# One group-norm chain for all four channel blocks in the last element of a two-layer attention kernel

## The chip, the cores and the metric

The kernel runs on one core of a Trainium2 chip. The metric is the device time of one execution in microseconds (us), as the median of three runs. Beside these runs there is one profiled execution with a trace; its span is the time from its first to its last recorded instruction.

The core's engines each have a queue of their own and work in its order: TensorE (PE, with its weight loads shown apart as PEld), VectorE (DVE), ScalarE (ACT), GpSimd (POOL) and SyncE (SP), which here only issues DMAs.

## The reference, cut to what matters

The input is eight images ("elements") of 512 channels and 32 x 32 = 1024 positions, in float32. Two attention layers follow each other; every element is computed by itself.

```python
# layer 0
hn  = group_norm(x, gn1_scale, gn1_bias)          # 32 groups of 16 channels
qkv = w_qkv @ hn + b_qkv                          # 8 heads of 64 channels
a   = softmax(q^T k / 8) applied to v, per head
out = w_proj @ a + b_proj
x   = x + group_norm(out, gn2_scale, gn2_bias)    # the second group norm
# layer 1: one head of 512 channels, with rows of weights normed and q, k, v divided by their rms
x   = (x + w_out @ attention(x)) / sqrt(2)
```

A group norm takes mean and variance over the 16 channels of a group and all positions, and then scales and shifts each channel. The change concerns the group norm of `out` and the sum with `x` at the end of layer 0.

## The kernel before

**Tiling.** The 512 channels are four blocks of 128 partitions (`CI` = 4); block j of a tile is `t[:, j, :]`, 128 x 1024. The positions fall into two halves of 512 (`th`), the width of one matmul. A float32 matmul shows as two records in the trace.

**Order of the work.** The order is written out by hand. Every engine is wrapped in `InOrder` (line 26), which pins each engine's instructions to the program's order, so all of them carry line 34 in the profile and are told apart by the names of their tiles. The loop over elements runs layer 0's heads in 32 steps, then the end of layer 0, then layer 1. In all elements but the last, the end of layer 0 is `finish_layer0` (line 691), which has matmuls of the next element to put between its steps. The last element has no next one, and ends layer 0 in another way.

**The last element's end of layer 0.** Its output projection is taken in shares. `project_out_half` (line 508) has already written the shares of blocks 0 and 1 of `a`, with the bias, into `o`, while the heads still ran. `OutBegun` (line 517) then starts the sums of block 2 of `a` for three of the four output blocks, in three PSUM tiles `pp` (all that the pool `ps_s`, line 101, has). After the last heads' values, `finish_last` (line 528) adds the rest: `project_out(j, th, pm)` gives PE the last share of output block j, and DVE adds the PSUM tile to `o`. Output block 3 was not begun; it takes both shares at once, and its PSUM tile is that of block 0, free when block 0 has been added to `o`.

**The second group norm, before.** In `finish_last` it is one chain for each block of channels, with one column each. `norm(j)` takes the statistics (two `bn_stats`, one `bn_aggr`, tiles `st` and `mv`). `GroupNorm.mean_steps` (line 261) lets PE average over the groups with a matmul against `gavg` (PSUM tile `pm`), and DVE does four small steps (`mean`, `d` three times). `GroupNorm.coeff_steps` (line 276) averages again on PE (`pv`); DVE adds the epsilon (`ve`), finds the reciprocal root by a start value and three rounds of four steps (`rsqrt_steps`, line 191), and ends with `a` and `c`. Then ACT applies `a` and `c` to block j of `o`, and DVE adds the block to `x`. The chains are interleaved with the projections: in round j, the first half of block j's projection comes first in the code, then the coefficients and the activation of block j-2, then the second half, the add of block j-2 to `x`, the add of block j to `o`, the means of block j-1, and the statistics of block j. The last two blocks' remains follow behind the loop, with the fetch of `gram` between them.

**What comes behind it.** `fetch("gram", b)` issues on SP the load of layer 1's first weights into the buffer that the projection's weights held (`places`, line 209: both have the tag `p`), so it waits for the last projection. `fetch("value", b)` (line 1092) comes next on SP. `Layer1.project` (line 750) starts with the products `py` of `gram` and `x`, block by block: output block cj takes blocks 0 to cj of `x`, 20 matmuls in all. DVE takes sums and differences of `x` (`RightSide.sums`, line 584) and multiplies `py` by `x` into `xy`, from which the rms comes. The products `p_u`, `p_v`, `p_e` and `po` follow.

Of the kernel before, what the change touches and what calls it, by code (L numbers as in the profile page):

```python
# [8 lines left out]
F32 = mybir.dt.float32  # L9
I32 = mybir.dt.int32  # L10
AF = mybir.ActivationFunctionType
ALU = mybir.AluOpType
AX = mybir.AxisListType
P = 128
# [4 lines left out]
G1S, G1B, BQ, BK, BV, BP, G2S, G2B, GQKV, GOUT, NCOLS = 0, 4, 8, 12, 16, 20, 24, 28, 32, 44, 48  # L19
# [33 lines left out]
def attention_blocks_kernel(  # L53
# [29 lines left out]
    CI, NT, HN = C // P, N // P, N // 2  # L83
# [15 lines left out]
    small = ctx.enter_context(tc.tile_pool(name="small", bufs=3))  # L99
# [4 lines left out]
    PE, VE, AC, PO, SY = (InOrder(tc, e) for e in (nc.tensor, nc.vector, nc.scalar, nc.gpsimd, nc.sync))  # L104

    def big(name, lead=CI):

        return slots.take([P, lead, CI * N // lead], name)

    def wide(name):  # L110
        return ps_s.tile([P, 2, HN], F32, tag="sc", name=name)
# [4 lines left out]
    def matmuls(pm, terms):  # L116

        for k, (lhsT, rhs) in enumerate(terms):
            PE.matmul(pm, lhsT, rhs, start=(k == 0), stop=(k == len(terms) - 1))
            if k % 2:  # L120
                yield

    def run(pieces):
        for _ in pieces:
            pass
# [105 lines left out]
    def fetch(name, b):  # L231
        SY.dma_start(out=place(name, b), in_=far[name])
# [16 lines left out]
    def gn_stats(st, src, k):  # L249
        VE.bn_stats(st[:, k, :], src[:, k * HN : (k + 1) * HN])  # L250
# [253 lines left out]
    def out_terms(a, j, th, cis):  # L504
        hs = slice(th * HN, (th + 1) * HN)
        return [(near["proj"][:, ci, j * P : (j + 1) * P], a[:, ci, hs]) for ci in cis]
# [21 lines left out]
    def finish_last(b, h, xt, o, begun):  # L528

        def project_out(j, th, pm):
            terms = out_terms(h.a, j, th, range(CI // 2, CI))
            if j in begun.pm:
                PE.matmul(pm[:, th, :], *terms[1], start=False, stop=True)
            else:
                run(matmuls(pm[:, th, :], terms))

        norms = {}

        def norm(j):
            st = small.tile([P, 2, 6], F32, tag="gn_st2", name=f"st2_{b}_{j}")
            mv = small.tile([P, 1, 2], F32, tag="gn_mv2", name=f"mv2_{b}_{j}")
            for k in range(2):
                gn_stats(st, o[:, j, :], k)
            VE.bn_aggr(mv[:, 0, :], st)
            norms[j] = GroupNorm(mv, 1, G2S + j, G2B + j, f"2_{b}_{j}")

        def apply(j):
            a, c = norms[j].coeffs()  # L550
            AC.activation(o[:, j, :], o[:, j, :], AF.Identity, bias=c, scale=a)

        def add(j):
            VE.tensor_add(xt[:, j, :], xt[:, j, :], o[:, j, :])

        for j in range(CI):
            pm = begun.pm[j] if j in begun.pm else wide(f"pp_{b}_{j}")
            project_out(j, 0, pm)
            if j > 1:
                apply(j - 2)  # L560
            project_out(j, 1, pm)
            if j > 1:
                add(j - 2)
            VE.tensor_add(o[:, j, :], o[:, j, :], pm.rearrange("p a f -> p (a f)"))
            if j:
                norms[j - 1].means()
            norm(j)
        apply(CI - 2)
        fetch("gram", b)
        add(CI - 2)  # L570
        norms[CI - 1].means()
        apply(CI - 1)
        add(CI - 1)
        slots.give(f"a_{b}")
        slots.give(f"o_{b}")

# [444 lines left out]
    for b in range(B):  # L1021
        hn, more = heads.hn, b + 1 < B
        todo = iter(())
        for i in range(STEPS):
            j, r = divmod(i, NB)
# [17 lines left out]
            if more:  # L1043
# [9 lines left out]
                k = i - 3 * CI - 2  # L1053
# [9 lines left out]
            if i == STEPS - NB + 1:  # L1063
                xt = big(f"x_{b}")
# [23 lines left out]
        if more:  # L1088
            finish_layer0(b, heads, rhs, xt, v0)
        else:  # L1090
            finish_last(b, heads, xt, o_last, begun)
# [59 lines left out]
```

## Time and profile before

| what | value |
|---|---|
| median of three runs | 3327.03 us (3325.53, 3327.03, 3331.03) |
| the profiled execution | 3326.53 us |
| its span | 3324.7 us |
| mean clock granted to PE in it | 0.997 |
| end of layer 0 of the last element, from the first add of `pp` to `o` until `py` starts | 3113.92 to 3144.45 us of the span |
| first products of layer 1 (`py`) | 3144.45, for 19.36 us |

The page gives busy times of the engines and groups of instructions. The answers from the trace give single instructions: start in the span, duration, engine, line, operation, output and inputs by name with their sizes, how often, and in brackets how long the engine was idle before and what ended that. An operation shown with 128x1 works on one column, with 128x4 on four.

### The profile page before, as it was taken

Reading aid. Unit: us, or ns where it says so; the run is one execution under the profiler, and the core shown is the slowest. Engines: PE = TensorE matmul, PEld = TensorE weight load, DVE = VectorE, ACT = ScalarE, POOL = GpSimd, SP = SyncE. Lnnn points to the kernel's source line nnn. Section 1 sums busy time; section 2 is a strip of 40 time slices with the busy share of each in tenths; the row PEclk is TensorE's granted clock in tenths of the full one; section 3 lists DMA queues with packets and bytes.
Section 4 is the critical chain, followed back from the end, with each engine's and each line's share of the span. In section 5 each row is a group of like instructions: output and inputs, shape, how many; then the busy total and the mean of one; then the engine's idle time right before and its main releaser. Section 6 shows DMA issues by size and latency. Waiting matters only on the chain.

```text
span 3324.7 us, 35644 instructions
## 1 busy us (share of the span) xinstructions
PE 3270.4 (98%) x13189; PEld 1608.1 (48%) x13189; DVE 2127.5 (64%) x2893; ACT 1069.8 (32%) x1811; POOL 981.4 (30%) x855
## 2 busy tenths in 40 slices
PE   7999999999999999999999999999999999999799
PEld 3544544445444454444544445444544445444354
DVE  4596646965479554885449754596646965478653
ACT  2353123521245212451215412254123531245210
POOL 0253123521245112450224503254123521234111
PEclk9999999999999999999999999999999999999899
DMA  5586205751068410782118811387204752067400
GB/s 187 160 212 189 76 13 155 195 176 67 7 185 209 147 45 26 204 224 95 45 50 217 236 47 44 88 216 199 76 13 142 200 166 93 5 159 203 151 7 25
DMA packets 182659, 411.86 MB, mean 124 GB/s; under 512 B 27444, under 2 KB 27480, under 8 KB 176344
## 3 DMA queue, kind: packets, MB, share of 16 engines
q1 hardware_dynamic: 182368, 409.58, 43.3%
q8 instruction: 105, 1.72, 0.2%
q14 instruction: 66, 0.54, 0.0%
q10 hardware_dynamic: 120, 0.02, 0.0%
HBM read 113.53 MB, written 27.56 MB: 42 GB/s over the span
## 4 chain that ended last, share of the span: by engine, by line
PE 86%; DVE 6%; DMA 5%; SPq 2%; issue 1%; ACT 0%; DVEq 0%; POOL 0%; POOLq 0%; ACTq 0%
PE po L34 24%; PE pqk L34 11%; PE s L34 11%; PE pv L34 7%; PE p_e_T L34 7%; PE p_e_B L34 5%; DMA pT<-pb 5%; PE py L34 4%; PE p_u_T L34 3%; PE p_o_T L34 3%; PE p_v_T L34 2%; PE p_u_B L34 2%; DVE pb L34 2%; PE p_o_B L34 2%; PE p_v_B L34 2%; SPq L34 2%
## 5 line engine op out<-in xcount | busy, mean ns | idle before, releaser
L34 ACT ACTIVATE p<-s,nm 128x1024 f32<-128x1024 f32 x512 | 565.5, 1109 | 861.3 <-DVE nm L34 825.7
L34 POOL TENSOR_SCALAR p<-p,tt 128x1024 f32<-128x1024 f32 x512 | 565.9, 1118 | 927.3 <-DVE tt L34 923.9
L34 DVE TENSOR_REDUCE nm<-s 128x1 f32<-128x1024 f32 x512 | 602.6, 1219 | 176.3 <-PE s L34 175.1
L34 DVE STREAM_TRANSPOSE pb<-p 128x2048 f32<-128x2048 f32 x256 | 589.6, 2303 | 23.2 <-POOL p L34 18.7
L34 PE MATMUL s<-qk 64*128 64x512 f32 x2048 | 508.1, 602 | 0.0
L34 PE MATMUL po<-pT,v 128*64 128x256 f32 x4096 | 470.3, 382 | 4.1 <-DMA pT<-pb 2.6
L34 PE MATMUL pqk<-hn,qk 64*128 64x512 f32 (+1 forms) x2016 | 473.9, 591 | 0.0
L34 PE MATMUL po<-e,v 128*128 128x512 f32 x1024 | 450.9, 595 | 0.0
L34 PEld LDWEIGHTS po<-pT,v 128*64 128x64 f32 x4096 | 286.7, 137 | 216.4 <-ACT v L34 71.3
L34 PEld LDWEIGHTS pqk<-hn,qk 64*128 64x128 f32 (+1 forms) x2016 | 201.8, 187 | 252.1 <-issue 239.7
L34 PEld LDWEIGHTS po<-e,v 128*128 128x128 f32 x1024 | 192.2, 190 | 252.7 <-issue 245.5
L34 POOL TENSOR_TENSOR u<-u,xy 128x512 f32<-128x512 f32 x64 | 78.9, 1270 | 781.3 <-DMA xy<-far_rinv 781.3
L34 PEld LDWEIGHTS s<-qk 64*128 64x128 f32 x2048 | 193.3, 186 | 238.6 <-issue 235.1
L34 PE MATMUL pv<-v,hn 128*128 128x512 f32 x512 | 230.7, 602 | 1.4 <-ACT v L34 1.4
L34 DVE TENSOR_TENSOR e<-e,p_e_T 128x512 f32<-128x512 f32 x160 | 107.1, 686 | 145.0 <-PE p_e_T L34 142.8
L34 POOL TENSOR_TENSOR qk<-qk,v 128x512 f32<-128x512 f32 x124 | 158.3, 1277 | 83.9 <-ACT v L34 83.9
L34 ACT ACTIVATE e<-e,shift,rinv 128x512 f32<-128x512 f32 x128 | 100.9, 811 | 247.7 <-DVE e L34 247.7
L34 POOL TENSOR_TENSOR esum<-esum,e 128x512 f32<-128x512 f32 x96 | 121.5, 1267 | 163.9 <-ACT e L34 161.4
L34 PEld LDWEIGHTS pv<-v,hn 128*128 128x128 f32 x512 | 95.3, 191 | 117.8 <-issue 116.0
L34 PE MATMUL p_e_T<-s,t 128*128 128x512 f32 x320 | 147.8, 592 | 0.0
L34 DVE TENSOR_TENSOR v<-po,esum 128x512 f32<-128x512 f32 x56 | 38.7, 691 | 160.0 <-PE po L34 159.8
L34 PE MATMUL py<-x,gram 128*128 128x512 f32 x320 | 140.7, 599 | 0.0
(184 smaller groups left out, 3077.8 us busy)
## 6 DMA issues: line engine op xcount, KB each, us to landing
pT<-pb SPq DMA_DIRECT2D x1024, 256.0 KB, 4.6
hn<-in_x_dram SPq DMA_DIRECT2D x32, 512.0 KB, 5.5
x<-in_x_dram SPq DMA_DIRECT2D x32, 512.0 KB, 5.8
out_dram<-x SPq DMA_DIRECT2D x32, 512.0 KB, 4.0
score<-far_score SPq DMA_DIRECT2D x8, 1792.0 KB, 7.5
value<-far_value SPq DMA_DIRECT2D x8, 1792.0 KB, 7.1
qk<-far_qk SPq DMA_DIRECT2D x7, 2048.0 KB, 8.1
proj<-far_proj SPq DMA_DIRECT2D x7, 1792.0 KB, 8.4
```

Source lines behind the costliest of these rows:

```text
L34: return lambda *args, **kw: self._pin(call(*args, **kw))
```

## The change

The four chains become one. In the loop over j, PE gets both halves of block j's projection one after the other, DVE adds the PSUM tile to `o` and takes the statistics of block j, into the columns of one `st` and one `mv` tile. Behind the loop come the fetch of `gram`, then one `GroupNorm` with four columns (one `pm`, one `pv`, each small DVE step once, 128 x 4), and last, for each block, the activation on ACT and the add to `x` on DVE. What is computed stays the same.

```diff
-        norms = {}
-
-        def norm(j):
-            st = small.tile([P, 2, 6], F32, tag="gn_st2", name=f"st2_{b}_{j}")
-            mv = small.tile([P, 1, 2], F32, tag="gn_mv2", name=f"mv2_{b}_{j}")
-            for k in range(2):
-                gn_stats(st, o[:, j, :], k)
-            VE.bn_aggr(mv[:, 0, :], st)
-            norms[j] = GroupNorm(mv, 1, G2S + j, G2B + j, f"2_{b}_{j}")
-
-        def apply(j):
-            a, c = norms[j].coeffs()
-            AC.activation(o[:, j, :], o[:, j, :], AF.Identity, bias=c, scale=a)
-
-        def add(j):
-            VE.tensor_add(xt[:, j, :], xt[:, j, :], o[:, j, :])
-
+        st = small.tile([P, CI, 2, 6], F32, tag="gn_st2", name=f"st2_{b}")
+        mv = small.tile([P, CI, 2], F32, tag="gn_mv2", name=f"mv2_{b}")
         for j in range(CI):
             pm = begun.pm[j] if j in begun.pm else wide(f"pp_{b}_{j}")
-            project_out(j, 0, pm)
-            if j > 1:
-                apply(j - 2)
-            project_out(j, 1, pm)
-            if j > 1:
-                add(j - 2)
+            for th in range(2):
+                project_out(j, th, pm)
             VE.tensor_add(o[:, j, :], o[:, j, :], pm.rearrange("p a f -> p (a f)"))
-            if j:
-                norms[j - 1].means()
-            norm(j)
-        apply(CI - 2)
+            for k in range(2):
+                gn_stats(st[:, j], o[:, j, :], k)
+            VE.bn_aggr(mv[:, j, :], st[:, j])
         fetch("gram", b)
-        add(CI - 2)
-        norms[CI - 1].means()
-        apply(CI - 1)
-        add(CI - 1)
+        norm = GroupNorm(mv, CI, G2S, G2B, f"2_{b}")
+        norm.means()
+        a, c = norm.coeffs()
+        for j in range(CI):
+            AC.activation(o[:, j, :], o[:, j, :], AF.Identity, bias=c[:, j : j + 1], scale=a[:, j : j + 1])
+            VE.tensor_add(xt[:, j, :], xt[:, j, :], o[:, j, :])
         slots.give(f"a_{b}")
         slots.give(f"o_{b}")
```

## The prediction

> **What bounds the kernel now.** I read the page first. Its busy line says that PE sets the time: it works in 98% of the span. So a stretch in which PE waits is worth its full length, as far as nothing later takes it back.
>
> ```profile
> PE 3270.4 (98%) x13189; PEld 1608.1 (48%) x13189; DVE 2127.5 (64%) x2893; ACT 1069.8 (32%) x1811; POOL 981.4 (30%) x855
> ```
>
> The change lies in the end of element 7 (the last one), so I then asked for busy time by stage around it. Columns: the stretch, its length, busy time and instructions of PE, PEld, DVE, ACT and POOL, the clock granted to PE, the DMA share and GB/s.
>
> ```profile
> 3112.00:3123.00 11.00, 8.44 (x22) 3.27 (x22) 8.30 (x29) 0.47 (x1) 0.00 (x0) 1.00 0.04 13
> 3123.00:3144.00 21.00, 5.44 (x12) 3.13 (x12) 15.48 (x57) 3.72 (x3) 0.00 (x0) 0.62 0.35 137
> 3144.00:3164.00 20.00, 20.00 (x43) 9.11 (x44) 14.81 (x32) 1.24 (x1) 0.00 (x0) 0.89 0.00 0
> ```
>
> From 3123 to 3144 us PE is busy for 5.44 of 21 us, and part of that is at half clock. DVE is busy for 15.48. This is one of the few places where PE does not set the pace. The timeline there (start, duration, engine, operation, idle time before and what ended it) tells why; I cut it to what the sums use:
>
> ```profile
> 3113.92 1.22 DVE L34 TENSOR_TENSOR o<-o,pp 128x1024 f32<-128x1024 f32 x1 [12.72 <-PE pp L34]
> 3115.17 1.29 DVE L34 BATCH_NORM_STATS2 st<-o 128x6 f32<-128x512 f32 x2
> 3116.49 0.21 DVE L34 BATCH_NORM_AGGREGATE mv<-st 128x2 f32<-128x12 f32 x1
> 3116.62 1.17 DVE L34 TENSOR_TENSOR o<-o,pp 128x1024 f32<-128x1024 f32 x1
> 3116.85 0.35 PE L34 MATMUL pm<-mv,gavg 128*128 128x1 f32 x2 [1.25 <-DVE mv L34]
> ...
> 3143.21 0.15 DVE L34 COPY mean<-pm 128x1 f32<-128x1 f32 x1
> ...
> 3144.00 0.58 PE L34 MATMUL pv<-d,gavg 128*128 128x1 f32 x2 [5.76 <-DVE d L34]
> ...
> 3144.45 19.36 PE L34 MATMUL py<-x,gram 128*128 128x512 f32 x40
> 3144.62 0.16 DVE L34 TENSOR_SCALAR ve<-pv 128x1 f32<-128x1 f32 x1 [0.68 <-PE pv L34]
> ...
> 3147.96 1.24 ACT L34 ACTIVATE o<-o,c,a 128x1024 f32<-128x1024 f32 x1 [5.92 <-DVE c L34]
> 3149.23 1.22 DVE L34 TENSOR_TENSOR x<-x,o 128x1024 f32<-128x1024 f32 x1 [1.37 <-ACT o L34]
> ```
>
> DVE's one queue holds four such chains one after the other. The tiny matmuls pm and pv of each stand in PE's queue ahead of what follows, so PE waits for DVE's queue. PE reaches py, the first product of the next layer, only behind the last pv at 3144.00. By then blocks 0 to 2 of x are ready; py runs through although block 3 of x is added only at 3149.23. So what sets the end is: DVE's chains, pv of block 3, py, and PE from there on. The chain of waits agrees: it goes through DVE and ACT from 3113.92 to 3143.79, then through pv, py, p_u and on along PE.
>
> **What the Trainium skill says.** "VectorE: DVE Perf Modes", section "The TRN2 errata — SBUF-src ops pay a fixed extra latency per instruction", says that a short operation costs a fixed time per instruction, whatever its width. The trace agrees: the small steps take 0.16 us with 1 column and 0.16 with 4. "TensorE: Matmul & The Clock Gate", Part 1, says that the clock is halved after an idle window of about 3.4 us and full again after about as much work. The trace agrees: behind a 5.76 us gap, py's first weight loads start 0.85 us apart, and 0.43 apart from 3148.63 on.
>
> **The change part by part.**
>
> *Removed.* Three of four chains. Each has 4 DVE steps before pv (mean, d three times) and 17 behind it (ve, one start value, 12 steps of refinement, 3 for a and c): 21 instructions every 0.193 us, 4.05 us; three are 12.2 us of DVE. Also three of four DVE waits for ACT between c and the add of x (1.31, 1.31, 1.37, 1.37 us; together 5.4), some 4 us. On PE, six of eight tiny matmuls go; what matters is that none stands between the projections.
>
> *The new path, clock by clock, from the same first instruction.*
> 1. PE: the projections' 20 records follow at 0.43 us. The first 8 end at 3115.6 as before; 12 more end at 3120.8. Block 3 needs the PSUM buffer that the add of block 0 frees at 3115.14, earlier than its turn at 3117.3: no wait.
> 2. DVE: add, two statistics and the aggregate of one block take 3116.62 - 3113.92 = 2.70 us. Block 3's aggregate starts at 3113.92 + 3 x 2.70 + 2.57 = 3124.59 and ends at 3124.80. The adds of blocks 2 and 3 fall at 3119.3 and 3122.0, later than their matmuls (3117.3 and 3120.8), so DVE never waits for PE here.
> 3. pm 0.15 us later as in block 0: 3124.95. I take the half-clock 0.62 us from pv to ve (3144.00 to 3144.62) for it: PE has been idle for 4.1 us. The copy of mean starts at 3125.57.
> 4. From that copy to pv: 3144.00 - 3143.21 = 0.79; pv at 3126.36, ve at 3126.98.
> 5. ve to ACT with one column: 3147.96 - 3144.62 = 3.34. Element 6 has the same chain with four columns:
>
> ```profile
> 2747.87 0.17 DVE L34 TENSOR_SCALAR a<-ve 128x4 int32<-128x4 int32 x1
> ...
> 2751.05 4.64 ACT L34 ACTIVATE o<-o,c,a 128x1024 f32<-128x1024 f32 x4 [2.48 <-DVE c L34]
> 2752.32 4.63 DVE L34 TENSOR_TENSOR x<-x,o 128x1024 f32<-128x1024 f32 x4 [1.31 <-ACT o L34]
> ```
>
> There it is 3.18 us from the start value to ACT, and 0.20 before it: 3.38. ACT starts at 3130.36.
> 6. The add of x block 0 comes 1.27 later, at 3131.63, and ends at 3132.85. PE starts py at about 3132.95 (0.1 for the hand-over is my allowance; aggregate to pm shows 0.15, d to pv 0.05).
>
> py starts 3144.45 - 3132.95 = 11.5 us earlier. Blocks 1 to 3 of x follow every 1.14 us (4.63 for four), the last ready at 3136.2. py's four records on block 0 alone last 4 x 0.85 = 3.4 us, to 3136.35: the later adds hide there. Without that cover py would wait up to 3.4 us.
>
> *The clock.* In the kernel before, pv opens PE's work at 3144.00 and full clock comes some 4.4 us later. In the new one py itself opens it, so about 0.45 us more of py is at half clock: 0.2 us lost. Gain left: **11.3 us**.
>
> *DVE beside py.* It must finish xy and the sums of each block. In element 6, where the adds also come in a bunch beside py, it waits for py before the products of blocks 1, 2 and 3 (0.51, 0.86 and 2.58 us). DVE is not the limit.
>
> *Moved DMAs.* SP's queue holds gram (1 MB) and then value (1.8 MB):
>
> ```profile
> 3131.54 0.33 SPq L34 DMA_DIRECT2D gram<-far_gram  x1
> 3131.97 0.38 SPq L34 DMA_DIRECT2D value<-far_value  x1
> ```
>
> gram takes the buffer of the projection weights and can start when their last matmul is done: 3131.5 before, about 3120.8 now, 10.7 us earlier. In the kernel before the DMA engines are quiet from 3140.0 on, so both transfers need at most 8.5 us: 3129.3 now, 3.6 us ahead of py. If gram alone came late, each microsecond past 3132.9 would be one. value is needed by p_v (3189.04 before); it moves 10.7 us and its user 11.3, with 49 us of slack. No issue passes another on SP.
>
> *Behind py* every step is the same as before and starts from py: p_u, the square sums, the two small transfers of 1/rms, value and weight products. PE carries all of it (154.79 busy of 161 us from 3164 on). So the 11.3 us come out at the end.
>
> **Sum.** The profiled execution has a span of 3324.7 and a time of 3326.53 us; 3324.7 - 11.3 = 3313.4 and 3326.53 - 11.3 = 3315.2. The median of the three runs is 0.5 above the profiled one: 3315.7. I predict **3315.6 us**, -0.34%.
>
> **Rivals.**
> - *py waits for the last block of x* (dependencies by whole tile, not by block): py starts at 3136.2 + 0.1, a gain of 7.9 us: 3319.1. Against it: before, py started at 3144.45, ahead of the last add at 3149.23.
> - *The clock* (the slower side). PE is now nearly idle from 3120.8 to 3132.9. Were the clock then halved for T us beyond the usual 4.4, T/2 is lost: the gain is gone at T = 23, and at T = 50 the kernel is 13.7 us slower: 3340.7. For it: "TensorE: Matmul & The Clock Gate", section "Seeing it yourself", tells of a clock seen stuck low for 50 us and more. Against it: before, PE did nothing but tiny pairs from 3131.5 to 3144.0, as long a stretch, and was at full clock 4.4 us later.
> - *The gain doesn't reach the end*: PE's later waits are for data that start from py, so only DMAs that start elsewhere could bind; value has 49 us. That, or the written order not being kept, gives about 3327.
>
> **How the numbers follow.** Main forecast 0.88; py behind the last block 0.05; no gain 0.03; the clock 0.04. A measurement of this kernel can tell about 0.2%, 6.65 us. Faster: the main case and most of the second, 0.91; same 0.05; slower 0.04. Bounds of the main case: if pm and pv run at full clock, 0.5 us less; if py does too, 2.4 less (five records x 0.43, and the 0.2): about 3312.7. Upwards the three runs before spread to 4 us over the median, and the second case lies at 3319.1. Range 3312.5 to 3319.6.
>
> **What would show it.** Right: four adds of o every 2.7 us with no small steps between; the projections' records without a gap, done by about 3121; one pm and one pv with 4 columns near 3125 and 3126.4; four activations in a row from 3130.4; py from 3133 to 3152.5; gram issued near 3121; everything behind at the same distances. Wrong: py far later than the first add of x, half-clock spacing of weight loads beyond 4.5 us, or a wait in p_v or p_e that was not there.

## The result, and the profile after

The changed kernel takes 3315.25 us (median of five runs, 3314.78 to 3318.06). The kernel before took 3328.38 us in the five runs that are compared with it. The ratio is 0.9963, with a 95% interval of 0.9953 to 0.9974: faster by 0.26 to 0.47%. The forecast was 3315.6 us and faster by 0.34%. The profiled execution of the changed kernel has a span of 3314.5 us and a time of 3316.36 us.

Busy time by stage of the changed kernel, with the columns as before (stretch, length, PE, PEld, DVE, ACT, POOL, PE's clock, DMA share, GB/s):

```profile
3123.00:3133.00 10.00, 1.18 (x4) 1.00 (x4) 6.60 (x26) 1.88 (x2) 0.00 (x0) 0.60 0.69 284
3133.00:3153.00 20.00, 19.28 (x39) 8.45 (x40) 14.87 (x17) 2.76 (x3) 0.00 (x0) 0.86 0.00 0
```

The stretch in which PE waits for the group norm is now 10 us long, where it was 21. DVE does 6.60 us of work in it instead of 15.48. `py` behind it has about kept its length: 19.90 us, for 19.36 before. The timeline of the same stage (start, duration, engine, operation, idle time before and what ended it):

```profile
3114.91 1.22 DVE L34 TENSOR_TENSOR o<-o,pp 128x1024 f32<-128x1024 f32 x1 [12.46 <-PE pp L34]
...
3121.77 0.33 SPq L34 DMA_DIRECT2D gram<-far_gram  x1
...
3125.43 0.21 DVE L34 BATCH_NORM_AGGREGATE mv<-st 128x2 f32<-128x12 f32 x1
3125.70 0.59 PE L34 MATMUL pm<-mv,gavg 128*128 128x4 f32 x2 [3.95 <-DVE mv L34]
3126.32 0.16 DVE L34 COPY mean<-pm 128x4 f32<-128x4 f32 x1 [0.68 <-PE pm L34]
...
3127.13 0.59 PE L34 MATMUL pv<-d,gavg 128*128 128x4 f32 x2 [0.84 <-DVE d L34]
...
3131.12 4.64 ACT L34 ACTIVATE o<-o,c,a 128x1024 f32<-128x1024 f32 x4 [17.65 <-DVE c L34]
3132.40 4.63 DVE L34 TENSOR_TENSOR x<-x,o 128x1024 f32<-128x1024 f32 x4 [1.31 <-ACT o L34]
3133.72 19.90 PE L34 MATMUL py<-x,gram 128*128 128x512 f32 x40 [6.00 <-issue]
...
3153.66 1.22 DVE L34 TENSOR_TENSOR xy<-py,x 128x1024 f32<-128x1024 f32 x1 [2.58 <-PE py L34]
```

One `pm` and one `pv` with four columns, one chain of small steps, four activations in a row, and four adds behind them. `py` starts 0.1 us after the first of the four adds has ended (3132.40 + 1.22 = 3133.62), while the other three still run until 3137.03. The last line is DVE's last product of `py` and x; in the kernel before it is this one:

```profile
3163.85 1.22 DVE L34 TENSOR_TENSOR xy<-py,x 128x1024 f32<-128x1024 f32 x1 [2.58 <-PE py L34]
```

To compare executions I measure from t0, the start of the first add of `pp` to `o`, because t0 itself lies at another time in each execution (3112.9 to 3116.9 us here). The same three distances, all to the starts of instructions, were read from every profile of this study:

| kernel | t0 to first `py` | t0 to DVE's last product of `py` and x | from there to the end of the span |
|---|---|---|---|
| before | 30.53 | 49.93 | 160.85 |
| changed | 18.81 | 38.75 | 160.84 |
| changed, profiled again | 18.83 | 38.65 | 160.83 |
| four chains, all late | 33.20 | 52.61 | 160.82 |
| projections first, four chains | 33.73 | 52.97 | 160.84 |
| the same, `pm` of block 0 ahead | 33.42 | 53.10 | 160.86 |
| the same, `pm` and `pv` of block 0 ahead | 30.54 | 49.80 | 160.85 |
| two chains of two columns | 20.18 | 40.49 | 160.81 |
| changed, adds in reverse order | 22.29 | 41.60 | 160.85 |
| changed, with fillers on PE | 18.48 | 35.92 | 160.81 |
| the same, block 0 in halves | 17.57 | 34.98 | 160.84 |

The last column settles one question at once: whatever this stage does, the rest takes 160.81 to 160.86 us. What is won or lost up to the last `py` reaches the end in full. The change wins 49.93 - 38.75 = 11.2 us there. In its profiled execution t0 came 1.0 us later than in that of before, so the spans differ by only 10.2 us. The medians differ by 13.1 us; the interval of the ratio, which is 8.7 to 15.6 us, holds both.

### The profile page after: what moved, and what is told of

Its sections match the earlier page's. It is cut to its first block, busy times and chain, and to the rows that moved or that the text cites. A ratio compares the mean times of both kernels' runs of the same rounds, so it can differ in the third digit from the quotient of the medians.

```text
span 3314.5 us, 35553 instructions
## 1 busy us (share of the span) xinstructions
PE 3267.3 (99%) x13177; PEld 1610.2 (49%) x13177; DVE 2117.2 (64%) x2830; ACT 1068.9 (32%) x1811; POOL 981.4 (30%) x855
## 4 chain that ended last, share of the span: by engine, by line
PE 89%; DVE 4%; DMA 4%; SPq 2%; issue 1%; ACT 0%; DVEq 0%; POOL 0%; POOLq 0%
PE po L34 25%; PE s L34 12%; PE pqk L34 12%; PE pv L34 7%; PE p_e_T L34 7%; PE p_e_B L34 5%; PE py L34 4%; DMA pT<-pb 4%; PE p_u_T L34 3%; PE p_o_T L34 3%; PE p_v_T L34 3%; PE p_u_B L34 2%; PE p_o_B L34 2%; PE p_v_B L34 2%; DVE pb L34 2%; SPq L34 2%
```

## The experiments

The theory: what PE waits for is DVE's queue of small steps, once for each chain, together with the tiny matmul pairs that stand in PE's queue ahead of `py`. One chain instead of four shortens that. The rivals: that it was the freeing of the projections from the tiny matmuls between them, or the earlier load of `gram`; or that something other than the first add of x releases `py`.

### Four chains, all begun late

This takes the change's late start alone and leaves the joining out.

```diff
-        norm = GroupNorm(mv, CI, G2S, G2B, f"2_{b}")
-        norm.means()
-        a, c = norm.coeffs()
         for j in range(CI):
-            AC.activation(o[:, j, :], o[:, j, :], AF.Identity, bias=c[:, j : j + 1], scale=a[:, j : j + 1])
+            norm = GroupNorm(mv[:, j : j + 1, :], 1, G2S + j, G2B + j, f"2_{b}_{j}")
+            norm.means()
+            a, c = norm.coeffs()
+            AC.activation(o[:, j, :], o[:, j, :], AF.Identity, bias=c, scale=a)
             VE.tensor_add(xt[:, j, :], xt[:, j, :], o[:, j, :])
```

> The change's late start without its joining: four chains with one column each, every one begun behind the last block's statistics. My theory (DVE's queue of small steps and the tiny matmul pairs ahead of py set the end): the first pv falls 12.2 us after the first add of pp to o, as after the change, and each later pv about 7.25 us behind the one before (4 steps 0.79, pv to ve 0.68, ve to ACT 3.34, ACT to the add of x 1.27, that add 1.14). The last pv is at 34.0 and py at 34.5 us behind the first add, where the kernel before has 30.5 and the changed one 18.8: about 4 us slower than before, 15.7 slower than the change; near 3332. Rival (the gain came from freeing the projections of the tiny matmuls between them): py early, a time near 3315.

Measured: 3331.01 us, ratio to before 1.0011 (1.0003 to 1.0019). Two lines of PE's timeline of this run:

```profile
3124.66 0.58 PE L34 MATMUL pv<-d,gavg 128*128 128x1 f32 x2 [4.45 <-DVE d L34]
...
3146.02 0.59 PE L34 MATMUL pv<-d,gavg 128*128 128x1 f32 x2 [6.15 <-DVE d L34]
```

The first and the last `pv` lie 21.36 us apart, three chains of 7.12 us (expected 7.25), and in front of each later one PE waits some 6 us for DVE's `d`. The first came 0.8 us earlier than expected, since `pm` of block 0 needs only block 0's statistics and had run long before. So `py` started 33.2 us behind t0 instead of 34.5. Late chains that stay separate are slower than the interleaved ones of before by 2.7 us in the stage. Here the late start is a cost, and the gain is in the joining.

### Two chains of two columns

```diff
-        norm = GroupNorm(mv, CI, G2S, G2B, f"2_{b}")
...
+        for h0 in (0, 2):
+            norm = GroupNorm(mv[:, h0 : h0 + 2, :], 2, G2S + h0, G2B + h0, f"2_{b}_{h0}")
+            norm.means()
+            a, c = norm.coeffs()
+            for i in range(2):
+                j = h0 + i
+                AC.activation(o[:, j, :], o[:, j, :], AF.Identity, bias=c[:, i : i + 1], scale=a[:, i : i + 1])
+                VE.tensor_add(xt[:, j, :], xt[:, j, :], o[:, j, :])
```

> The changed kernel with two chains of two columns, both behind the last block's statistics: the dose between one chain and four. My theory: the first pv at 12.2 us behind the first add of pp to o; then ve to ACT 3.4, ACT to the add 1.3, two adds 2.3, four steps of the second chain 0.8, so the second pv at about 20.6 and py at 21.1, 2.3 us later than the change's 18.8. Blocks 2 and 3 of x come at 27.1 and 28.2, while py works on blocks 0 and 1 until about 28, so no wait there: 2 to 3 us slower than the change. Rival (it is the number of instructions on DVE that counts, wherever they stand): 22 more steps of 0.195 us and one more wait for ACT, 5.5 us slower.

Measured: 3318.48 us, ratio 0.9973 (0.9962 to 0.9983). The first add and `py` in this run:

```profile
3115.30 1.22 DVE L34 TENSOR_TENSOR o<-o,pp 128x1024 f32<-128x1024 f32 x1 [13.45 <-PE pp L34]
...
3135.48 20.27 PE L34 MATMUL py<-x,gram 128*128 128x512 f32 x40
```

`py` starts 20.18 us behind t0, 1.4 us later than in the change, and its last product follows 1.7 us later. The expectation was 2.3 us; nearly all of the difference is the same 0.8 us as above, for here too the first `pm` need not wait for the last block. The rival's 5.5 us is refuted: of the second chain only the four steps ahead of its `pv` hold up `py`, and the 17 behind it run beside `py`.

### Projections first, chains as before

This frees the projections and brings `gram` forward, but leaves the four chains and DVE's order as they were.

```diff
...
+        for j in range(CI - 1):
+            for th in range(2):
+                project_out(j, th, pms[j])
+        add_o(0)
+        pms[CI - 1] = wide(f"pp_{b}_{CI - 1}")
+        for th in range(2):
+            project_out(CI - 1, th, pms[CI - 1])
         for j in range(CI):
...
-            project_out(j, 0, pm)
             if j > 1:
                 apply(j - 2)
-            project_out(j, 1, pm)
-            if j > 1:
                 add(j - 2)
...
             if j:
+                add_o(j)
                 norms[j - 1].means()
             norm(j)
```

This is shown against the kernel before. Behind the projections, DVE, ACT and the tiny matmuls keep their order of before; `add_o(j)` is the add of `pp` to `o`.

> The kernel before with one thing moved: PE gets all projections first and then the tiny matmuls; DVE and ACT keep their order, with four interleaved chains. My theory: DVE's queue is as long as before, so py starts within 0.5 us of 30.5 us behind the first add of pp to o, and the time is that of before, within 2 us, although gram is issued some 10 us earlier. Rival (the tiny matmuls that held up the projections, or the late gram, cost the time): py about 11 us earlier, near 3316.

Measured: 3331.33 us, ratio 1.0012 (1.0005 to 1.0019). `gram` was issued 6.9 us behind t0 instead of 17.6, and `py` started at 33.7. Both rivals are refuted as the cause: with free projections and an early `gram`, but four chains, `py` does not come earlier. But my own expectation missed too: the kernel is 3.2 us slower in the stage, not equal. DVE's timeline of this run:

```profile
3115.60 1.17 DVE L34 TENSOR_TENSOR o<-o,pp 128x1024 f32<-128x1024 f32 x1
3119.88 0.16 DVE L34 COPY mean<-pm 128x1 f32<-128x1 f32 x1 [3.11 <-PE pm L34]
```

I had kept DVE's order and forgotten what it waits for. `pm` of block 0 now stood behind all projections in PE's queue, and DVE idled for 3.11 us until it came. Two further runs test that this is the whole reason. The first puts only this `pm` back, ahead of the projection of block 2:

```diff
+        means = norms[0].mean_steps()
+        next(means)
         project_block(2)
         pms[CI - 1] = wide(f"pp_{b}_{CI - 1}")
         project_block(CI - 1)
...
-        norms[0].means()
+        run(means)
```

It is shown against the run just told, with the first rounds of its loop written out: `project_block(j)` is both halves of block j's projection, and `next(means)` issues `pm` alone.

> The kernel with all projections first, but pm of block 0 put back ahead of the projection of block 2; the other tiny matmuls stay behind the projections, DVE and ACT keep their order. In the run without this, the copy of mean waited 3.11 us, for pm stood behind twelve more records of the projections. If that wait is all that made it slower than before, it is gone here: py at 30.5 us behind the first add of pp to o (within 0.5), and the time of before within 1 us on the same way (3.2 us less than with pm behind). If the order of the projections itself costs something, py stays at 33 us or more.

Measured: 3329.7 us, ratio 1.0004 (0.9996 to 1.0013), and `py` still at 33.4. That is a miss again. The wait has not gone but moved one step on, from `mean` to `ve`, because `pv` of block 0 too stood behind the projections:

```profile
3117.93 0.15 DVE L34 COPY mean<-pm 128x1 f32<-128x1 f32 x1
...
3122.84 0.16 DVE L34 TENSOR_SCALAR ve<-pv 128x1 f32<-128x1 f32 x1 [2.74 <-PE pv L34]
```

The second run puts `pv` of block 0 back too, ahead of the projection of block 3:

```diff
         project_block(2)
+        run(means)
+        norm(1)
+        coeffs = norms[0].coeff_steps()
+        next(coeffs)
         pms[CI - 1] = wide(f"pp_{b}_{CI - 1}")
         project_block(CI - 1)
-        run(means)
-        norm(1)
+        run(coeffs)
...
```

`next(coeffs)` issues `pv` alone; the steps behind it, the activation and the add to x of block 0 keep their order on DVE and ACT.

> As the run with pm of block 0 ahead of the projection of block 2, but pv of block 0 is put back ahead of the projection of block 3 too. In that run DVE's wait had only moved from the copy of mean to ve (2.74 us, for pv stood behind the projections). Now block 3's projection no longer waits for the later tiny matmuls, and nothing of block 0's chain waits for the projections. If PE's order matters to this stage only by what DVE waits for, py is back at 30.5 us behind the first add of pp to o (within 0.3), the last product of py and x at 49.9, and the time is that of before within 1 us on the same way, with gram issued some 8 us earlier than before. If the early projections themselves cost time or save it, py is elsewhere.

Measured: 3327.97 us, ratio 1.0000 (0.9992 to 1.0008), with `py` at 30.54 and its last product at 49.80, as in the kernel before, although `gram` is issued 8.8 us earlier behind t0:

```profile
3114.75 1.22 DVE L34 TENSOR_TENSOR o<-o,pp 128x1024 f32<-128x1024 f32 x1 [12.17 <-PE pp L34]
...
3145.29 19.23 PE L34 MATMUL py<-x,gram 128*128 128x512 f32 x40
```

So PE's order counts in this stage through what DVE waits for, and an earlier `gram` is worth nothing by itself. In the changed kernel the order of the projections and the tiny matmuls is no question: its only chain starts when the projections are long done. The early `gram` it probably needs: issued 17.6 us behind t0 as before, it would have had 1.2 us until `py` at 18.8, and in the kernel before the loads of `gram` and `value` together ended some 8.5 us after the issue. That is argued from these numbers; a changed kernel with a late `gram` was not tried.

### The adds to x in reverse order

```diff
-        for j in range(CI):
+        for j in reversed(range(CI)):
```

> The changed kernel with the four activations and the four adds to x in the order of blocks 3, 2, 1, 0. If py's start waits for block 0 of x alone, it moves by three adds of 1.14 us: from 18.8 to 22.2 us behind the first add of pp to o, and the time is 3.3 us longer than the change's. If py waits for all blocks anyhow, or for gram, or for something else that is later than the first add, nothing changes.

Measured: 3319.76 us, ratio 0.9975 (0.9966 to 0.9985). The two lines that show it, from the timeline of this run:

```profile
3134.41 4.63 DVE L34 TENSOR_TENSOR x<-x,o 128x1024 f32<-128x1024 f32 x4 [1.37 <-ACT o L34]
3139.14 19.27 PE L34 MATMUL py<-x,gram 128*128 128x512 f32 x40 [9.48 <-issue]
```

The four adds end at 3139.04, and `py` follows 0.1 us later: 22.29 us behind t0 instead of 18.81, three adds later. So the add of block 0 of x releases `py`, whichever place it has; that it is not simply the last add is shown by the changed kernel, where three adds still run beside `py`. The profile itself names no releaser there ("issue"); the moved add does. The last product comes only 2.85 us later than in the change, since `py` reached full clock sooner in this run.

### Fillers while PE waits

Twelve matmuls whose products nothing reads stand where PE waits: five ahead of `pm`, seven behind `pv`.

```diff
+        def filler(n, name):
+            pf = wide(name)
+            for _ in range(n):
+                PE.matmul(pf[:, 0, :], root2, h.a[:, 0, :HN], start=True, stop=True)
+
+        filler(5, f"pf_{b}_0")
         norm.means()
-        a, c = norm.coeffs()
+        steps = norm.coeff_steps()
+        next(steps)
+        filler(7, f"pf_{b}_1")
+        run(steps)
+        a, c = norm.a, norm.c
```

The changed kernel ran again beside it, as the measure.

> The changed kernel again, as the measure for the run beside it: 11 to 13 us faster than before.

> The changed kernel with twelve filler matmuls on PE, whose products nothing reads: five between the last projection and pm, seven between pv and the first py, as long as PE waits there. They should keep PE at full clock. If the half clock after the gap costs what my sum says, py takes 17.3 us in place of 19.9, and pm and pv about 0.25 us less each: 3 us faster than the change, some 15 faster than before. If the clock is full for another reason or falls anyhow, py takes 19.9 us as in the change and the time is the same; if the fillers run at half clock and end late, py starts later and the time is longer.

Measured: 3316.91 us for the changed kernel (ratio 0.9967, 0.9954 to 0.9979), 9.8 us less than before and so under the 11 to 13 that I expected, while its stage again gains 11.3 us (49.93 - 38.65); and 3312.90 us with fillers (0.9959, 0.9946 to 0.9973). PE's timeline with fillers:

```profile
3126.09 6.25 PE L34 MATMUL pf<-a,root 128*128 128x512 f32 x14
3132.25 17.41 PE L34 MATMUL py<-x,gram 128*128 128x512 f32 x40
```

`py` takes 17.41 us, where it takes 19.78 in the changed kernel profiled beside it. It starts 0.35 us earlier behind t0, because `pm` and `pv` answer sooner: DVE waits 0.54 and 0.48 us for them instead of 0.68 each. Together the last product of `py` comes 2.7 us earlier. Busy time by stage gives the clock granted from 3133 to 3150 us as 1.00; in the changed kernel it was 0.86 from 3133 to 3153. The two intervals of the whole times overlap, so the whole times alone would not tell the two kernels apart; the stage does, in one profile of each.

### Block 0 of x in halves

On top of the fillers (six instead of seven behind `pv`), block 0 is applied and added in two halves.

```diff
+        first = (slice(0, HN), slice(HN, N))
         for j in range(CI):
-            AC.activation(o[:, j, :], o[:, j, :], AF.Identity, bias=c[:, j : j + 1], scale=a[:, j : j + 1])
-            VE.tensor_add(xt[:, j, :], xt[:, j, :], o[:, j, :])
+            for s in (slice(0, N),) if j else first:
+                AC.activation(o[:, j, s], o[:, j, s], AF.Identity, bias=c[:, j : j + 1], scale=a[:, j : j + 1])
+                VE.tensor_add(xt[:, j, s], xt[:, j, s], o[:, j, s])
```

> The kernel with filler matmuls (six in place of seven behind pv), with block 0 of o applied and added to x in two halves of 512 columns, so that the first product of py can start behind the first half. From rows of this kernel: ACT on 512 columns 0.8 us in place of 1.24, the add 0.69 in place of 1.22. py starts 0.9 us earlier, 17.6 us behind the first add of pp to o in place of 18.5, and the last product of py and x follows at about 35.0 in place of 35.9; the time is about 1 us less than with fillers alone. If the later blocks of x, each some 0.4 us later, hold up py at full clock, the gain is smaller or gone.

Measured: 3312.03 us, ratio 0.9951 (0.9939 to 0.9964). `py` starts 17.57 us behind t0 and its last product follows at 34.98, both as expected. It has the shortest stage of the study: 3.8 us less than the change, 15.0 us less than before. Its interval of the whole time still overlaps that of the change.

## Why the prediction was right

**The bound.** The waits that ended last were DVE's chains and the tiny pairs ahead of `py`. The four late chains, the two chains and the one chain show it as a dose: 33.2, 20.2 and 18.8 us until `py`. The dose is not proportional: with two or four chains `py` follows the last `pv`, and with one it waits for the rest of the chain and the add of block 0 too.

**Steps 1 and 2.** The projections ran without a gap and `gram` was issued 6.86 us behind t0 (forecast 6.9). The last aggregate started 10.52 us behind t0; the forecast was 10.67. The blocks follow each other by 2.70, 2.65 and 2.65 us, not three times 2.70, and the last aggregate by 2.52 us on its add, not 2.57.

**Steps 3 to 5.** Half clock for `pm` and `pv` was the right choice: both show 0.59 us, where block 0's `pm` before took 0.35 at full clock, and DVE waits 0.68 for each. `pm` came 0.06 us behind the aggregate, where I had taken 0.15 from block 0. Together with the 0.15 us from step 2 this makes up the error at ACT, which started 16.21 us behind t0, for 16.44 forecast. The durations of element 6's four-column chain carried over as they were.

**Step 6.** `py` started 18.81 us behind t0, for 19.03. The hand-over of 0.1 us, an allowance and not worked out, was right to the last digit, and the reversed order shows that it is the add of block 0 that counts.

**The clock: the term that was mis-sized.** I let half clock cost 0.2 us more than before. From its start to the last product, `py` took 19.40 us before and 19.94 after: 0.54 us. The weight loads of the changed kernel show when full clock came:

```profile
3138.12 0.34 PEld L34 LDWEIGHTS py<-x,gram 128*128 128x128 f32 x1 [0.52 <-DVE t L34]
3138.86 0.19 PEld L34 LDWEIGHTS py<-x,gram 128*128 128x128 f32 x1 [0.41 <-issue]
3139.29 0.19 PEld L34 LDWEIGHTS py<-x,gram 128*128 128x128 f32 x1 [0.24 <-issue]
```

Loads that last 0.19 us and follow each other by 0.43 began 5.1 us after `py`'s start, where I had counted 4.4. The reason that I gave, a `pv` that opens PE's work 0.45 us ahead of `py` and so ends the half clock sooner, is not borne out. With two chains a `pv` stands just as close ahead of `py`, and the short loads began 5.9 us after `py`'s start. With the adds in reverse order no `pv` is near, and they began after 4.1 us. Over all kernels without fillers it was 3.6 to 5.9 us. "TensorE: Matmul & The Clock Gate", Part 1, says that the window which decides runs freely, so that the moment varies. It puts this at 500 ns either way; the spread here is wider, 2.4 us, and the measurement decides. That the window is the reason is not shown by any run. From `py`'s start to the last product it makes 19.24 to 20.31 us without fillers, and 17.41 and 17.44 with them.

**What was luck.** The two errors, 0.2 us too late at `py` and 0.3 us too little for the clock, nearly cancelled, so that 11.3 us forecast met 11.2 measured; with a clock as in the two-chain run it would have been 0.4 us less. And that 3315.6 us met 3315.25 is closer than the runs allow: the medians differ by 13.1 us, and by 9.8 when the changed kernel ran again, where the stage gives 11.2 and 11.3.

**The rivals.** `py` did not wait for the last block of x. The clock was full again 5.1 us after `py`'s start, so nothing near the 23 us came that would have eaten the gain. DVE kept up: it waited for `py` (2.58 us ahead of the last product), and `py`, once begun, not for it. And the gain reached the end: the rest took 160.84 us, as before.

## What to carry to other kernels

The small dependent steps here cost by the instruction and not by the column: 0.16 us each with one column and with four. If several such chains share one queue with the work that feeds them, it can pay to join them into one, even if that one starts later: here that gained 11.2 us, while the same late start with separate chains cost 2.7. When an order is changed on one engine, list what the other engines wait for in it: here a tiny matmul behind dense ones cost DVE 3.1 us, and the wait moved to the next tiny matmul when the first was put right. A dense stage behind a dependent chain can start at half clock, as `py` did here; twelve matmuls that nobody reads, placed in the wait, brought 2.4 us of it back.

## What the runs showed that I had not expected

The length of the half clock differs from profile to profile: the same 40 records and DVE's last product took 19.24 to 20.31 us from `py`'s start in the kernels without fillers, with no rule that these runs show. The two profiles of the changed kernel differ by only 0.12 us. The place where the profiles differ most is ahead of this stage: t0 varied from 3112.9 to 3116.9 us over eleven profiles, although nothing was changed there. In the kernel before, the chain of waits reaches PE's last share through a transfer of `pT` that ended at 3107.10 us. In three of the runs, the one with the latest t0 among them, PE did not wait at that place. Why t0 varies was not tried and stays open.
